# Expert blocks of 256 rows become 57 of 256 and 21 of 128, with an expert's weights packed side by side in DRAM

## The chip, the cores and the metric

The kernel runs on one core of a Trainium2 chip. A core has five engines that run their own instruction lists: PE (TensorE, matrix products into PSUM; its weight loads are listed apart as PEld), DVE (VectorE), ACT (ScalarE), POOL (GpSimd) and SP (SyncE, which here only issues transfers). The transfers themselves run on 16 DMA engines. The metric is the device time of one execution in microseconds, from which a profile of one execution is taken as well.

## The reference

A layer norm, then attention and a mixture of experts side by side, both added to the input. The input has 32 sequences of 256 rows of 128 numbers (8192 rows), all in f32.

```python
def attention(xn, Wqkv, Wproj, bproj):      # 16 heads of 8, rotary, window of 64, causal
    q, k, v = heads(xn @ Wqkv.T); q, k = rotary(q), rotary(k)
    attn = softmax(where(allow, q @ k.T / sqrt(8), -inf))
    return merge(attn @ v) @ Wproj.T + bproj

def experts(xn, gate_w, gate_b, w1, b1, w2, b2):   # 8 experts, hidden 512
    weights, indices = top_k(xn @ gate_w.T + gate_b, 2)
    weights = softmax(weights)
    out = 0
    for e in range(8):
        w_e = sum(weights * (indices == e), keepdims=True)
        h = gelu(xn @ w1[e] + b1[e])          # erf form
        out = out + w_e * (h @ w2[e] + b2[e])
    return out

xn = layernorm(x)
return x + attention(xn) + experts(xn)
```

## The kernel before

Each row goes to two of the eight experts, so 16,384 rows of expert work have to be spread. The kernel sorts rows by expert through DRAM and works them off in blocks.

**Attention** (class `Attention`) takes the sequences one after another, four turns each (`run`, L787 to L862); turn (z, r) is the r-th of sequence z. PE's order is written by hand. Beside it runs the generator `beside` (L1037), which `turn` (L805) advances once per turn: it puts normalisation, routing, sorting, experts and collecting between the attention's instructions. Steps that `yield False` go on in every turn; those that `yield True` take a share of a small budget.

SP's queue is in order. In turn (z, 1) it gets the four `km` loads of the next sequence, in (z, 2) the four `qm` loads (`alone`, L574), each set of 32 KB transfers waiting for the rotated k or q from DVE (`rk`, `rq`, L571).

**Routing and sorting.** `route` (L306), four times for a quarter of the rows each, finds each row's two experts and its place (`slot`) in the expert's region of `xs_d` in DRAM, `ER` = 8192 + 256 rows per expert. `scatters` (L1070) sends rows there with indirect DMAs from POOL, two a turn; a row of `xs_d` is 130 numbers: 128 of the row, then the row of `ys_d` to which its result goes, and its weight. When the last quarter is routed, `blocks` (L378) computes from the region ends how many blocks of 256 each expert has and, for 71 blocks, the expert (`exps[0]`) and the first row (`exps[1]`); `fills` (L1051) writes 256 void rows behind each region. 71 blocks suffice for any routing: 64 full ones and 7 more for the rests; unused ones work on void rows.

**The experts** (`experts`, L909) come when all scatters are out, in one piece, with attention standing still in between. For block b:

- `load(b)` (L916), on SP: two numbers are read into registers (expert e, first row r), then four transfers: `xg` (256 rows, 130 KB), `w1` (256 KB, 2 KB per partition), `w2` (256 KB, four runs of 512 B per partition), `b2` (one row broadcast to 128 partitions, 64 KB). The tiles have 5 buffers each; four blocks are loaded before the first, then block b + 4 is requested after the down of block b - 1.
- `turn(b)` (L935): two PE transposes into `pxg`, a DVE copy to `xT` (L940), a small DVE copy of the target rows and weights to `at` (L942, 4 buffers).
- `up(b)` (L945): four products of 128x128 weights with 256 columns into `ph` (L952; f32, two instructions each), ACT gelu with the bias of the block's expert to `h` (L958).
- `down(b)` (L964): eight products with `h` as weights and 128 columns each (L970, 16 instructions) into `po` (one PSUM buffer); DVE adds `b2` (L975) and multiplies by the weight (L976); POOL sends the two halves with indirect DMAs to the rows of `ys_d` that `at` names (L981).

PE's order of one iteration is: transposes of b + 1, up of b, down of b - 1. In the profile w1 and w2 are both called `w`, `b2` is `b`, the result tile is `yg`.

**Collecting** (`collect`, L1010): back in attention's turns, SP reads `ys_d` in order, POOL adds it to `x`, SP writes the output.

Of the kernel before, what the change touches and what calls it, by code (L numbers as in the profile page):

```python
# [12 lines left out]
I32 = mybir.dt.int32  # L13
# [18 lines left out]
NB = 71  # L32
ER = 8192 + BT
# [17 lines left out]
C_ROW = C_BLK + NB  # L51
C_VOID = C_ROW + 128
C_ALL = C_VOID + 30
# [3 lines left out]
def constants():  # L57

    f = np.float32
    c = np.zeros((P, C_ALL), f)  # L60
    p = np.arange(P)
    e = np.arange(NE)
    c[:, C_PRE : C_PRE + P] = p[:, None] < p[None, :]
    c[:, C_TIE : C_TIE + NE] = NE - e
    c[:, C_NUM : C_NUM + NE] = e
    c[:, C_BLK : C_BLK + NB] = np.arange(NB)
    c[:, C_ROW : C_ROW + 128] = p[:, None] + P * np.arange(128)[None, :]
    c[:, C_BASE : C_BASE + NE] = ER * e
    c[:, C_RUN : C_RUN + 17 * NE] = np.arange(17 * NE) % 17 > 0
    v = np.arange(30)[None, :]  # L70
    c[:, C_VOID : C_VOID + 30] = 2 * 8192 + BT * (v // 2) + 2 * p[:, None] + v % 2

    r = (p % HB)[:, None]
    k = np.arange(2 * HB)[None, :]
    ok = (k >= r) & (k <= r + WIN)
    c[:, C_MQ : C_MQ + 2 * HB] = np.where(ok & (k >= HB), f(0), f(NEG))
    c[:, C_MQ + 2 * HB : C_MQ + 4 * HB] = np.where(ok, f(0), f(NEG))

    q = np.arange(HB)[None, :]
    c[:, C_MK : C_MK + HB] = np.where(q >= r, f(0), f(NEG))  # L80
    c[:, C_MK + HB : C_MK + 2 * HB] = np.where(q <= r, f(0), f(NEG))
    c[:, C_MK + 2 * HB : C_MK + 3 * HB] = NEG
    for i in range(4):
        at = C_PICK + HB * i
        c[:HB, at : at + HB] = np.eye(HB, dtype=f)
        c[HB + 3 * i : HB + 3 * i + 3, at : at + HB] = 1
    half = HD // 2
    inv = f(1.0) / f(ROPE_BASE) ** (np.arange(half, dtype=f) / f(half))
    freq = np.arange(T, dtype=f)[None, :] * inv[p % 32 // 8][:, None]
    c[:, C_COS : C_COS + T] = np.cos(freq)  # L90

    c[:, C_SIN : C_SIN + T] = np.sin(freq) * np.where(p % 8 < 4, f(-1), f(1))[:, None]
    return c, np.zeros((P, 2 * P), f)
# [3 lines left out]
def tile_layer(  # L97
# [23 lines left out]
    NI = NB - 2 * B * T // BT  # L121
# [68 lines left out]

    xs_d = tc.dram_tile([NE * ER + NI * BT, ROW], F32, name="xs_d")
    ys_d = tc.dram_tile([2 * B * T + (NE + NI) * BT, D], F32, name="ys_d")
# [185 lines left out]
    def blocks(rt, misc):  # L378
# [4 lines left out]
        def temp(name, shape, dtype=F32):  # L383
            return rt.tile(shape, dtype, tag=name, name=name)

        after, base = run[:, :, GN], c[:, C_BASE : C_BASE + NE]
        nc.vector.tensor_copy(ends, after[0:1, :])
        nb_i = temp("nb_i", [P, NE], I32)
        nc.vector.scalar_tensor_tensor(nb_i, after, float(BT - 1), base, ALU.add, ALU.subtract)
        nc.vector.tensor_single_scalar(  # L390
            nb_i, nb_i, BT.bit_length() - 1, ALU.arith_shift_right
        )
        nb = temp("nb", [P, NE])
        nc.vector.tensor_copy(nb, nb_i)

        f = temp("f", [P, 3, NE])
        nc.vector.tensor_tensor_scan(f[:, 1, :], ones[:, 0:NE], nb, 0.0, ALU.mult, ALU.add)
        nc.vector.tensor_sub(f[:, 0, :], f[:, 1, :], nb)

        idle = NE * ER - (NB - NI) * BT  # L400
# [3 lines left out]
        nc.vector.tensor_scalar_add(f[:, 2, :], f[:, 2, :], -float(idle))  # L404
        yield False
        pf = misc("pf")
        for k in range(3):
            nc.tensor.matmul(
                pf[0:NE, k : k + 1], lhsT=f[:, k, :], rhs=ident[:, 0:1], start=True, stop=True
            )  # L410
        nc.tensor.matmul(
            pf[0:NE, 3:4], lhsT=c[:, C_NUM : C_NUM + NE], rhs=ident[:, 0:1], start=True, stop=True
        )
        fT = temp("fT", [NE, 4])
        nc.vector.tensor_copy(fT, pf[0:NE, 0:4])

        blk = c[0:NE, C_BLK : C_BLK + NB]
        oh = temp("ohb", [NE, NB])
        nc.vector.tensor_scalar(oh, blk, fT[:, 0:1], None, ALU.is_ge)
        nc.vector.scalar_tensor_tensor(oh, blk, fT[:, 1:2], oh, ALU.is_lt, ALU.mult)  # L420
        yield False
        pn = misc("pn")
        for k in range(2):
            nc.tensor.matmul(
                pn[0:1, k * NB : (k + 1) * NB], lhsT=fT[:, 3 - k : 4 - k], rhs=oh,
                start=True, stop=True,
            )
# [3 lines left out]
        for k in range(NHC):  # L431
# [7 lines left out]
        at = temp("at", [1, NB])  # L439
        nc.vector.tensor_scalar(  # L440
            at, c[0:1, C_BLK : C_BLK + NB], float(BT), float(idle), ALU.mult, ALU.add
        )
        nc.vector.tensor_add(exps[:, 1, :], at, nums[:, 1, :])
# [465 lines left out]
    def experts():  # L909
        with (  # L910
# [5 lines left out]
            def load(b):  # L916
                e = nc.sync.value_load(exps[0:1, 0, b : b + 1], min_val=0, max_val=NE - 1)
                r = nc.sync.value_load(
                    exps[0:1, 1, b : b + 1], min_val=0, max_val=NE * ER + (NI - 1) * BT
                )  # L920
                x = wt.tile([P, 2, ROW], F32, tag="xg", name=f"xg{b}")
                nc.sync.dma_start(
                    out=x, in_=xs_d[bass.ds(r, BT), :].rearrange("(p n) d -> p n d", n=2)
                )
                a = wt.tile([P, H], F32, tag="w1", name=f"w1_{b}")
                nc.sync.dma_start(out=a, in_=w1[bass.ds(e, 1), :, :].rearrange("o d h -> (o d) h"))
                z = wt.tile([P, NHC, D], F32, tag="w2", name=f"w2_{b}")
                nc.sync.dma_start(
                    out=z, in_=w2[bass.ds(e, 1), :, :].rearrange("o (k p) d -> p (o k) d", p=P)
                )  # L930
                bias = wt.tile([P, D], F32, tag="b2", name=f"b2_{b}")
                nc.sync.dma_start(out=bias, in_=b2_d[bass.ds(e, 1), :].to_broadcast([P, D]))
                return x, a, z, bias

            def turn(b, x):  # L935
                pt = misc(f"pxg{b}")[:, 0:BT]
                for n in range(2):
                    nc.tensor.transpose(pt[:, n * P : (n + 1) * P], x[:, n, 0:D], ident)  # L938
                xT = io.tile([P, BT], F32, tag="xT", name=f"xgT{b}")
                nc.vector.tensor_copy(xT, pt)  # L940
                at = io.tile([P, 2, 2], I32, tag="at", name=f"at{b}", bufs=4)
                nc.vector.tensor_copy(at, x[:, :, D:].bitcast(I32))  # L942
                return xT, at

            def up(b, xT, a):  # L945
                h = hid.tile([P, NHC, BT], F32, tag="h", name=f"h{b}")
                for k, tag in ((0, "sh"), (2, "sl")):
# [3 lines left out]
                    for j in range(2):  # L951
                        nc.tensor.matmul(  # L952
                            ph[:, j * BT : (j + 1) * BT],
                            lhsT=a[:, (k + j) * P : (k + j + 1) * P], rhs=xT,
                            start=True, stop=True,
                        )
                    for j in range(2):
                        nc.scalar.activation(  # L958
                            h[:, k + j, :], ph[:, j * BT : (j + 1) * BT], AF.Gelu,
# [4 lines left out]
            def down(b, h, z, bias, at):  # L964
                po = ps_y.tile([P, 4, P], F32, tag="y", name=f"po{b}").rearrange(
                    "p s t -> p (s t)"
                )[:, 0 : 2 * D].rearrange("p (n d) -> p n d", n=2)
                for n in range(2):
# [5 lines left out]
                y = io.tile([P, 2, D], F32, tag="y", name=f"yg{b}", bufs=4)  # L974
                nc.vector.tensor_add(y, po, bias.unsqueeze(1).to_broadcast([P, 2, D]))  # L975
                nc.vector.tensor_mul(  # L976
                    y, y, at[:, :, 1:2].bitcast(F32).to_broadcast([P, 2, D])
                )
                for n in range(2):
# [10 lines left out]
            ahead = [load(b) for b in range(4)]  # L990
            yield
            yield
            (xT, at), last = turn(0, ahead[0][0]), None
            for b in range(NB):
                x, a, z, bias = ahead.pop(0)
                now, to = xT, at
                if b + 1 < NB:
                    xT, at = turn(b + 1, ahead[0][0])
                h = up(b, now, a)
                if last is not None:  # L1000
                    down(*last)
                if b + 4 < NB:
                    ahead.append(load(b + 4))
                last = (b, h, z, bias, to)
# [32 lines left out]
    def beside():  # L1037

        rt = early.enter_context(tc.tile_pool(name="rt", bufs=1))
        void = rt.tile([P, NE, 2, ROW], F32, tag="void", name="void")  # L1040
        nc.gpsimd.memset(void, 0.0)

        def fill(first, n):

            at = C_VOID + 2 * first
            nc.gpsimd.tensor_copy(
                void[:, 0:n, :, D].bitcast(I32),
                c[:, at : at + 2 * n].rearrange("p (n k) -> p n k", k=2),
            )

        def fills():  # L1051
# [3 lines left out]
            for e in range(NE):  # L1055
                end = nc.sync.value_load(
                    ends[0:1, e : e + 1], min_val=ER * e, max_val=ER * (e + 1) - BT
# [3 lines left out]
                        out=xs_d[bass.ds(end, BT), :].rearrange("(p n) d -> p n d", n=2),  # L1061
                        in_=void[:, e],
# [29 lines left out]
        def go_on(entry):  # L1092
            entry[2] = next(entry[1], None)
            if entry[2] is None:
# [7 lines left out]
                out=xs_d[rows : rows + NI * BT, :].rearrange("(j p n) d -> p j n d", p=P, n=2),  # L1102
# [5 lines left out]
        while next(transfers, transfers) is not transfers:  # L1108
# [3 lines left out]
            if (z, r) == (1, 1):  # L1112
                begin("masks1", att.masks(1))

# [68 lines left out]
```

## Time and profile before

| what | value |
|---|---|
| median of 4 runs | 795.41 us (792.66, 792.78, 798.04, 798.21) |
| profiled execution | 791.79 us, span 790.0 us, granted clock 0.991 |
| PE busy | 732.2 us, 93% |
| PEld busy | 477.4 us, 60% |
| DVE busy | 498.6 us, 63% |
| ACT busy | 381.2 us, 48% |
| POOL busy | 413.6 us, 52% |
| first transpose of the experts to the last down's end | 359.42 to 632.31 us |
| DMA queue of SP (q1) | 117,344 packets, 79.64 MB |
| DMA queue of POOL (q0) | 8,640 packets, 17.84 MB |

The slices of a page cut the span into 40 equal parts and give the busy share in tenths. A line of a timeline has the start in us, the time from the first start to the last end of the merged instructions, engine, line, operation, output and inputs, how many were merged, and in brackets the idle time before and what ended it. Starts and ends of matmuls overlap, since they are pipelined; a step's time is read from start to start. A line of the waits has the waiting instruction, what it waited for, total us, times, and the longest.

### The profile page before, as it was taken

The numbers are of one execution on the slowest core, as the hardware profiler recorded it, in microseconds if no ns is written. First come the engines' busy times: TensorE is split into PE (matmuls) and PEld (weight loads), VectorE is DVE, ScalarE is ACT, GpSimd is POOL, SyncE is SP. The second block draws the span as 40 slices with busy tenths as digits, with TensorE's granted clock in tenths as the row PEclk, the third lists the DMA queues.
The fourth block names the chain that finished last, engine by engine and source line by source line (L and its number), as shares of the span: only waits on it lengthen the run. The fifth ranks groups of instructions, "written<-read, shape, count | busy, mean of one in ns | idle before, by whom it ended". The sixth has DMA issues, their size and how long they took to land.

```text
span 790.0 us, 20453 instructions
## 1 busy us (share of the span) xinstructions
PE 732.2 (93%) x7524; PEld 477.4 (60%) x7524; DVE 498.6 (63%) x1163; ACT 381.2 (48%) x695; POOL 413.6 (52%) x668
## 2 busy tenths in 40 slices
PE   3899989999989999998999999999999999999995
PEld 2344444444444444446999998999999944444442
DVE  3658968898887888874333433333333377878763
ACT  4256455465556454454444444444444444454543
POOL 2301568567878737781555555555555544444300
PEclk9999989999999999999999999999999999999999
DMA  4700111111112101316887888887887355436100
GB/s 134 203 24 8 49 38 52 51 39 54 59 42 65 56 28 51 119 55 198 226 233 224 230 228 241 229 246 231 222 245 228 105 146 150 141 106 169 42 22 15
DMA packets 126372, 98.87 MB, mean 125 GB/s; under 512 B 14648, under 2 KB 112600, under 8 KB 126272
## 3 DMA queue, kind: packets, MB, share of 16 engines
q1 hardware_dynamic: 117344, 79.64, 36.1%
q0 software_dynamic: 8640, 17.84, 6.5%
q8 instruction: 60, 0.98, 0.5%
q14 instruction: 40, 0.33, 0.1%
q10 hardware_dynamic: 288, 0.08, 0.0%
HBM read 65.09 MB, written 24.02 MB: 113 GB/s over the span
## 4 chain that ended last, share of the span: by engine, by line
PE 64%; DVE 14%; ACT 10%; DMA 4%; issue 3%; SPq 2%; POOL 2%; DVEq 0%; ACTq 0%; POOLq 0%
PE po L970 14%; PE ph L952 14%; PE sl L703 8%; ACT pr L713 7%; PE sl L689 7%; PE sh L634 6%; DVE mx L648 4%; PE sh L622 4%; PE y L725 4%; ACT xn L283 2%; PE pxg L938 2%; PE pm L672 1%; PE pg L295 1%; DMA ys_d<-yg,at 1%; DVE yt L734 1%
## 5 line engine op out<-in xcount | busy, mean ns | idle before, releaser
L713 ACT ACTIVATE pr<-sl 128x1024 f32<-128x1024 f32 x128 | 130.7, 1022 | 193.1 <-PE sh L634 184.9
L981 POOL DMA_INDIRECT ys_d<-yg,at x142 | 137.2, 967 | 131.1 <-DVE yg L976 98.9
L648 DVE TENSOR_REDUCE mx<-sh 128x8 f32<-128x1024 f32 x128 | 156.3, 1221 | 69.8 <-PE sh L634 69.4
L958 ACT ACTIVATE h<-ph,b_b 128x256 f32<-128x256 f32 x284 | 116.4, 470 | 147.8 <-PE ph L952 147.8
L634 PE MATMUL sh<-km,rq 32*64 32x512 f32 x1024 | 148.6, 641 | 0.5 <-DMA km<-rk 0.5
L457 POOL DMA_INDIRECT xs_d<-xn,slot x128 | 127.2, 994 | 35.8 <-issue 19.2
L703 PE MATMUL sl<-qm,rk 32*64 32x256 f32 (+1 forms) x1280 | 142.6, 485 | 0.0
L970 PEld LDWEIGHTS po<-w,h 128*128 128x128 f32 x1136 | 138.0, 192 | 4.3 <-issue 0.7
L970 PE MATMUL po<-w,h 128*128 128x128 f32 x1136 | 138.4, 275 | 0.6 <-issue 0.6
L952 PE MATMUL ph<-xgT,w 128*128 128x256 f32 x568 | 135.9, 383 | 0.6 <-DVE xgT L940 0.4
L952 PEld LDWEIGHTS ph<-xgT,w 128*128 128x128 f32 x568 | 103.3, 192 | 12.4 <-DVE xgT L940 0.7
L689 PE MATMUL sl<-rs,pick_i 76*64 76x512 bf16 x512 | 80.4, 390 | 26.2 <-ACT pr L713 20.8
L975 DVE TENSOR_TENSOR yg<-po,b 128x256 f32<-128x256 f32 x71 | 30.2, 425 | 84.7 <-PE po L970 80.9
L725 PE MATMUL y<-pr,vst 128*32 128x128 f32 (+1 forms) x1536 | 70.1, 315 | 1.0 <-DVE yt L734 1.0
L703 PEld LDWEIGHTS sl<-qm,rk 32*64 32x64 f32 x1280 | 47.9, 131 | 37.9 <-issue 29.1
L942 DVE COPY at<-xg 128x4 int32<-128x4 int32 x71 | 14.3, 202 | 83.9 <-issue 60.4
L725 PEld LDWEIGHTS y<-pr,vst 128*32 128x32 f32 x1536 | 40.1, 110 | 44.3 <-issue 39.0
L677 ACT COPY rs<-pm 12x1024 bf16<-12x1024 bf16 x63 | 60.2, 1000 | 10.8 <-PE pm L672 10.3
L689 PEld LDWEIGHTS <-pick_i 76*64 76x64 bf16 x512 | 26.9, 108 | 58.7 <-issue 46.5
L622 PE MATMUL sh<-mq,unit 64*64 64x512 bf16 x512 | 54.4, 414 | 4.1 <-DVE mx L648 3.7
L622 PEld LDWEIGHTS <-unit 64*64 64x64 bf16 x512 | 15.7, 104 | 57.7 <-issue 57.3
L734 DVE STREAM_TRANSPOSE yt<-y 128x512 f32<-128x512 f32 x64 | 45.3, 708 | 4.5 <-PE y L725 4.5
(143 smaller groups left out, 845.2 us busy)
## 6 DMA issues: line engine op xcount, KB each, us to landing
w<-in_L_ffn_w_dram SPq DMA_DIRECT2D x142, 256.0 KB
xg<-xs_d SPq DMA_DIRECT2D x71, 130.0 KB
yc<-ys_d SPq DMA_DIRECT2D x32, 256.0 KB
b<-b_d SPq DMA_DIRECT2D x71, 64.0 KB
qm<-rq SPq DMA_DIRECT2D x128, 32.0 KB
out_dram<-x SPq DMA_DIRECT2D x32, 128.0 KB
km<-rk SPq DMA_DIRECT2D x126, 32.0 KB
x<-in_L_attn_x_dram SPq DMA_DIRECT2D x15, 256.0 KB
```

The source lines that it names most:

```text
L457: nc.gpsimd.indirect_dma_start(out=xs_d, out_offset=bass.IndirectOffsetOnAxis(ap=slot[:, n, k : k + 1], axis=0), in_=xns[n // NT][:, n % N ...
L622: nc.tensor.matmul(ps[HB * h : HB * h + HB, ii, :, :], lhsT=unit2[half, :], rhs=mq[half, which, :].unsqueeze(1).to_broadcast([HB, 4, 2 * HB]),
L634: nc.tensor.matmul(ps[HB * h : HB * h + HB, ii, :, :], lhsT=q[r, t * HB : (t + 1) * HB], rhs=km[r, :, t * HB : (t + 2) * HB], start=False, ...
L648: nc.vector.tensor_reduce(mx, ps, AX.X, ALU.max, negate=True)
L689: nc.tensor.matmul(ps[HB * e : HB * e + HB, ii, :, :], lhsT=pick_i[:, 2 * ip + ii, :], rhs=rs[e][:, :, n * P : (n + 1) * P], start=True, s ...
L703: nc.tensor.matmul(ps[HB * e : HB * e + HB, ii, :, lo:hi], lhsT=k[r, kt * HB : (kt + 1) * HB], rhs=qm[r, :, n * P + lo : n * P + hi], star ...
L713: nc.scalar.activation(pr, ps, AF.Exp, scale=1.0 / math.sqrt(HD))
L725: nc.tensor.matmul(py[32 * i : 32 * i + 32, 2 * o : 2 * o + 2, lo:hi], lhsT=self.vsts[z % 3][:, tile_, i, o, :], rhs=q["pr", n, i // 2][:, ...
L952: nc.tensor.matmul(ph[:, j * BT : (j + 1) * BT], lhsT=a[:, (k + j) * P : (k + j + 1) * P], rhs=xT, start=True, stop=True,)
L958: nc.scalar.activation(h[:, k + j, :], ph[:, j * BT : (j + 1) * BT], AF.Gelu, bias=b1_b[:, k + j, b : b + 1],)
L970: nc.tensor.matmul(po[:, n, :], lhsT=h[:, k, n * P : (n + 1) * P], rhs=z[:, k, :], start=(k == 0), stop=(k == NHC - 1),)
L981: nc.gpsimd.indirect_dma_start(out=ys_d, out_offset=bass.IndirectOffsetOnAxis(ap=at[:, n, 0:1], axis=0), in_=y[:, n, :], in_offset=None,)
```

## The change

- The row count of a block is 256 (`BT`) for blocks 0 to 56 and 128 (`HT`) for blocks 57 to 77. `blocks` hands out whole blocks of 256 first, up to 57 over all experts, and covers what is left with half blocks; it computes both kinds' ranges, in one step more (a further `yield False`). An expert's region ends in 128 void rows instead of 256, and `fills` writes half as much.
- The order of work spreads the half blocks evenly: fifteen times three whole and a half one, six times two whole and a half one. The last block is a half one.
- A new generator `pack`, begun at turn (3, 0), copies for each expert w1, w2 and b2 (broadcast to 128 rows) into `w_d` in DRAM, 1152 numbers (4608 B) per partition: three DRAM to DRAM transfers per expert, 24 in all, on SP's queue; two in one turn, one in the next.
- `load` issues two transfers instead of four: `xg` and one tile `w` of 576 KB from `w_d`. `up` and `down` take their weights and the bias from slices of `w`, which has 5 buffers as w1, w2 and b2 had.
- `turn`, `up` and `down` take the row count from the tile: a half block has one transpose, up products of 128 columns, four down products, one scatter.

The diff, cut to its core:

```diff
-NB = 71
-ER = 8192 + BT
+NF, NHB, NHU = 57, 21, 14
+NB = NF + NHB
+HT = BT // 2
+ER = 8192 + HT
+NI = NHB - NHU
...
+    w_d = tc.dram_tile([NE, P, WROW], F32, name="w_d")
...
+        whole, halves = steps_of("whole", 0, BT), steps_of("halves", HT - 1, HT)
...
+        bounds(0, whole)
...
+        yield False
+        got = temp("got", [P, 2, NE])
+        nc.vector.tensor_single_scalar(got, f[:, 0:2, :], float(NF), ALU.min)
+        nc.vector.tensor_sub(whole, got[:, 1, :], got[:, 0, :])
+        nc.vector.scalar_tensor_tensor(halves, whole, -2.0, halves, ALU.mult, ALU.add)
+        bounds(3, halves)
...
             def load(b):
                 e = nc.sync.value_load(exps[0:1, 0, b : b + 1], min_val=0, max_val=NE - 1)
+                n = 2 if b < NF else 1
...
-                x = wt.tile([P, 2, ROW], F32, tag="xg", name=f"xg{b}")
+                x = wt.tile([P, 2, ROW], F32, tag="xg", name=f"xg{b}")[:, 0:n]
                 nc.sync.dma_start(
-                    out=x, in_=xs_d[bass.ds(r, BT), :].rearrange("(p n) d -> p n d", n=2)
-                )
-                a = wt.tile([P, H], F32, tag="w1", name=f"w1_{b}")
-                nc.sync.dma_start(out=a, in_=w1[bass.ds(e, 1), :, :].rearrange("o d h -> (o d) h"))
-                z = wt.tile([P, NHC, D], F32, tag="w2", name=f"w2_{b}")
+                    out=x, in_=xs_d[bass.ds(r, n * P), :].rearrange("(p n) d -> p n d", n=n)
+                )
+                w = wt.tile([P, WROW], F32, tag="w", name=f"w{b}")
                 nc.sync.dma_start(
-                    out=z, in_=w2[bass.ds(e, 1), :, :].rearrange("o (k p) d -> p (o k) d", p=P)
-                )
-                bias = wt.tile([P, D], F32, tag="b2", name=f"b2_{b}")
-                nc.sync.dma_start(out=bias, in_=b2_d[bass.ds(e, 1), :].to_broadcast([P, D]))
-                return x, a, z, bias
+                    out=w, in_=w_d[bass.ds(e, 1), :, :].rearrange("o p d -> (o p) d")
+                )
+                return x, w
...
                         nc.tensor.matmul(
-                            ph[:, j * BT : (j + 1) * BT],
-                            lhsT=a[:, (k + j) * P : (k + j + 1) * P], rhs=xT,
+                            ph[:, j * BT : j * BT + t],
+                            lhsT=w[:, (k + j) * P : (k + j + 1) * P], rhs=xT,
                             start=True, stop=True,
                         )
...
+            order, n = [], 0
+            for b in range(NF):
+                order.append(b)
+                while (n + 1) * NF <= (b + 1) * NHB:
+                    order.append(NF + n)
+                    n += 1
...
+        def pack():
+            for e in range(NE):
+                yield False
+                nc.sync.dma_start(out=w_d[e, :, 0:H], in_=w1[e])
+                nc.sync.dma_start(
+                    out=w_d[e, :, H : H + NHC * D].rearrange("p (k d) -> p k d", d=D),
+                    in_=w2[e].rearrange("(k p) d -> p k d", p=P),
+                )
+                yield False
+                nc.sync.dma_start(
+                    out=w_d[e, :, H + NHC * D :], in_=b2_d[e : e + 1, :].to_broadcast([P, D])
+                )
...
+            if (z, r) == (3, 0):
+                begin("pack", pack())
```

## The prediction

> **What bounds the kernel now.** I read the page's slices first, then the chain, then the expert stage by stretches, by PE and SP in order of time, and last who waits.
>
> ```profile
> PE   3899989999989999998999999999999999999995
> PEld 2344444444444444446999998999999944444442
> DMA  4700111111112101316887888887887355436100
> ```
>
> The slices show three stages: attention with routing, from slice 18 to 31 the experts (PE and its weight loads both full), then attention again. The diff works in the middle one.
>
> ```profile
> PE 64%; DVE 14%; ACT 10%; DMA 4%; issue 3%; SPq 2%; POOL 2%; DVEq 0%; ACTq 0%; POOLq 0%
> ...
> 500.00:550.00 50.00, 50.00 (x348) 47.20 (x348) 18.64 (x55) 22.31 (x55) 28.31 (x53) 1.00 0.83 235
> ```
>
> Chain by engine, and one stretch of the experts (busy PE, PEld, DVE, ACT, POOL, clock, DMA share, GB/s): PE has no gap, at full granted clock; the next fullest are the DMA engines, 0.83.
>
> ```profile
> 438.00 0.38 PE L938 MATMUL pxg<-ident,xg 128*128 128x128 f32 x2
> 438.22 1.89 PE L952 MATMUL ph<-xgT,w 128*128 128x256 f32 x8
> 439.95 1.95 PE L970 MATMUL po<-w,h 128*128 128x128 f32 x16
> 441.74 0.38 PE L938 MATMUL pxg<-ident,xg 128*128 128x128 f32 x2
> ```
>
> PE in order of time: start to start, one block is 0.22 (transposes) + 1.73 (up) + 1.78 (down) = 3.73 us. An instruction of 256 columns takes 1.73/8 = 216 ns, one of 128 takes 1.78/16 = 111 ns.
>
> ```profile
> 427.21 0.33 SPq L922 DMA_DIRECT2D xg<-xs_d  x1
> 427.74 0.33 SPq L926 DMA_DIRECT2D w<-in_L_ffn_w_dram  x1
> 428.31 0.38 SPq L928 DMA_DIRECT2D w<-in_L_ffn_w_dram  x1
> 428.93 0.33 SPq L932 DMA_DIRECT2D b<-b_d  x1
> 430.74 0.33 SPq L922 DMA_DIRECT2D xg<-xs_d  x1
> ```
>
> SP in order of time: a block's four issues and two register loads take 3.53 us, hardly less than PE's 3.73. Pairing starts, xg is issued only 2.4 to 4 us before its transposes in blocks 4 to 33. SP is a second bound close behind PE.
>
> ```profile
> 471.91 0.44 PE L938 MATMUL pxg<-ident,xg 128*128 128x128 f32 x2 [0.15 <-DMA xg<-xs_d]
> ...
> 487.92 0.44 PE L938 MATMUL pxg<-ident,xg 128*128 128x128 f32 x2 [0.87 <-DVE at L942]
> ```
>
> ```profile
> DVE at L942 <- DMA ys_d<-yg,at: 23.3, 23, 3.0
> ...
> PEld pxg L938 <- DMA xg<-xs_d: 2.1, 4, 1.1
> ```
>
> PE's few stalls in order of time, and two rows of the waits (total us, times, longest): from the transposes of block 3 (369.60) to those of block 70 (622.32) are 252.72 us, 67 x 3.73 = 249.98 of it work, so 2.7 us of stalls, at late xg loads and at late copies of `at`. That copy waits for earlier scatters to land.
>
> **The change part by part.** *Rows.* Before 71 x 3.73 = 264.9. A half block has 1 transpose, 8 up and 8 down instructions of 128 columns: 17 x 0.111 = 1.89. After: 57 x 3.73 + 21 x 1.89 = 252.3. **-12.5 us**, all on PE, the bound. The price of its up matmuls is L970's row, same shape, weights also changed every time.
>
> A rule speaks against that: the Trainium skill, "TensorE: Matmul & The Clock Gate", part 3, has weight loads overlap running matmuls only where their row groups differ, and these fill all rows. The rows here disagree: 216 ns for 256 columns and 111 for 128 leave 216 - 2 x (216 - 111) = 6 ns for anything that doesn't scale with columns.
>
> *One transfer.* SP saves two issues of about 0.57 (427.74 to 428.93 by starts): 3.53 - 1.15 = 2.4 us a load, while the mean block needs 252.3/78 = 3.23 of PE. Unmerged, 78 x 3.53 = 275 would have bound. In the compiled order each SP DMA waits for the eighth before it: two blocks in flight before, four after. So loads run ahead until a buffer is missing. The one tile w is now held until the add of its block, where w1 was free after the up: w for four blocks on is issued about 0.6 into the iteration after that add's matmuls, three iterations (9.35 at the shortest) less 0.4 ahead of its up; xg some 1.9 behind on SP, 6.9 ahead of its transposes. Both beat today's 2.4 to 4, so the load stalls go: **-2.0** of the 2.7. Without that cover each us of lateness costs up to 78.
>
> *DMA time.* Between 400 and 500 us the SP queue's share, 71.1% of 1600 engine-us for 27 blocks, is 42.1 a block. Full-load stretches give packets of 496 B 32.5 ns (20 to 30 us: 5603 at 113.7%), of 1 KB 46 (34 to 37 us), of 3.8 KB 150 (6 to 7 us: 104, 0.40 MB, 97.4%; 25.7 GB/s an engine). After: whole 128 x 46 ns + 0.59 MB/25.7 = 28.8, half 27.1; in sum 2211 engine-us for 2989. At today's 17.2 GB/s it would be 55 MB/17.2 = 3200, with 135 scatters of 2.84 still 89% of 16 x 252. No bound either way: 0.
>
> *The index ring.* `at` has four buffers: block i's copy waits for the scatters of block i-4, and behind it on DVE stands the add that frees the one PSUM buffer the next down needs. By starts, the copies of blocks 6 to 70 ran 5.07 to 8.28 us after the transposes of block i-1 (median 6.32). PE stalls only past two iterations + 1.95 - 0.6 (copy, add) = 8.8: never so far. With a half block among them iterations shrink to 2.89 and 2.84, the limit at 24 places to 7.0 to 7.1, elsewhere to 7.8 or more. Laying the 65 measured delays on these limits gives 24 x 0.1 + 0.3 = 2.7 us of stalls. A late copy delays the add and the scatters behind it, so I take **+4**; bounds 0.7 (all landing 0.5 earlier) and 16 (1.0 later).
>
> *Ends.* SP's faster first loads save 0 to 1.5 at xg 1's 1.44 us wait (the ACT table load follows); the last block's 0.56 gap has a longer down above it: **-1**.
>
> *Before the experts.* 24 pack DMAs go to SP among the km and qm issues, about 0.6 each, 14 us over 16 turns of 3.4; SP waits there 175 us for rk anyway. Their data, 5120 packets of 512 B and 1024 of 2 KB (83 ns between the rows above), is 251/16 = 16 us of DMA where the share is 0.16. A km load is issued three turns, 10 us, ahead and needs 2.4 + 2, so what stands before it (two transfers, 1.7) is hidden; without that cover up to 16. Eleven small DVE instructions of 0.11 to 0.29 in `blocks` add 2 us to an engine 85% busy there; its extra turn lies under the last 16 turns of scatters. **+1** (0 to 4). Smaller fills and 7 fewer scatters on POOL (0.97 each, POOL half idle): 0.
>
> Sum: -12.5 - 2.0 + 4 - 1 + 1 = **-10.5**. Profiled execution: 791.8 (span 790.0) - 10.5 = 781.3. The four runs lie near 792.7 and 798.1, their median 3.6 above that execution: 784.9 on that scale. I forecast **783**.
>
> **The rivals.** *A, slower: scatters land later.* Place: the ring. A load's queue will hold 8 packets of 4.6 KB an engine, about 8 x 0.18 = 1.4 us, issued just as the block's scatters go out. If a scatter stands behind all of them, delays shift by 1.0 to 1.5 and the ring's stalls are 16 to 30: from 1.0 on (12.5 + 2.0 + 1 - 1 = 14.5 to lose) it decides; at 1.5, 791.8 - 14.5 + 30 = 807. For it: landing already varies from 1.5 to 4.7 us after POOL's end. Against: 26% less DMA time, and the second scatter goes out 1.3 after the first, past the burst. The Trainium skill, "DMA: Bandwidth & Descriptors", "Queues, rings and completion order", has engines alternate between queues packet by packet; by it a scatter's two packets an engine wait 2 x 0.18, shift about 0.3, 2 us more than forecast. No row separates the two.
>
> *B, no gain: a milder shift.* At +0.7 the ring's list gives 10 us, 14 with its echo: 791.8 - 14.5 + 14 = 791.
>
> *C, the half block isn't half.* If each of its up matmuls showed a weight load as long as its own columns, up would cost a whole one's 1.73: 21 x 0.84 = +17.6, so 781.3 + 17.6 = 799. L970's row is against it.
>
> *D, more.* The lighter queue lands scatters 0.5 sooner, no load is late: -12.5 - 2.7 + 0.7 - 1.5 = -16, 776.
>
> **How the numbers follow.** Forecast (8 to 14 us less) 0.54, D 0.12, B 0.14, A 0.15, C 0.05. About 1% is what measurements of this kernel tell from no change. Faster by over that: forecast and D, 0.66; within it B and a part of A, 0.18; slower A's rest and C, 0.16. The range runs from D, 776 less the spread of runs, to A where it begins to cost: 775 to 796; the likeliest case alone gives 778 to 787.
>
> **What would show it.** Half blocks 1.89 us of PE by the timeline, ph of 128 columns at 111 ns; SP pace 2.4 and xg issued over 6 us ahead; PE idle before po or ph ending at DVE, just behind half blocks, 3 to 5 us in all; DMA share under 0.75; the stage 273 us before, 262 after; stretches before 357 us unchanged. Wrong it is if the waits of `at` on ys_d double and their longest exceeds 4 us (A), or if PE idles at km loads during the pack.

## The result and the profile after

The changed kernel takes 794.72 us (median of 42 runs, 781.55 to 808.94), the kernel before 793.79 beside it (63 runs, 789.27 to 803.39). The medians lie 0.9 us apart, the changed kernel's the longer: nothing was gained where 10.5 us were forecast. The ratio, 0.9951 with a 95% interval of [0.9929, 0.9973], takes of each kernel only the runs within 1.5% of its fastest, 15 of these 42 and 61 of these 63, and so flatters the kernel with the wider spread; the ratios further down are made the same way. The changed kernel's profiled execution took 797.46 us, span 795.7.

| us, profiled execution | before | after |
|---|---|---|
| up to the experts' first transpose | 359.4 | 361.6 (+2.1) |
| from there to the last down's end | 272.9 | 271.0 (-1.9) |
| the rest | 157.7 | 163.2 (+5.5) |
| span | 790.0 | 795.7 (+5.7) |

The slices of the changed kernel's page, busy tenths:

```profile
PE   3899989999989998998999799998999999999986
DMA  4701425111211101218877677877888355543100
```

In the expert stage PE now has a 7 and an 8 where it was full before, while DMA is no fuller. Slices 4 to 6 of DMA, counted from 0 as in the prediction, show the packing's copies. The chain by engine, then the same stretch of 50 us as before (busy PE, PEld, DVE, ACT, POOL, clock, DMA share, GB/s):

```profile
PE 54%; DVE 15%; ACT 10%; DMA 10%; issue 7%; POOL 3%; SPq 1%; DVEq 0%; POOLq 0%; ACTq 0%
```

```profile
500.00:550.00 50.00, 47.90 (x343) 44.76 (x341) 17.21 (x58) 22.71 (x62) 26.56 (x52) 1.00 0.80 246
```

PE lost ten points of the chain, DMA won six, and PE stands 2.1 of 50 us. PE in order of time, where nothing waits:

```profile
468.44 0.38 PE L971 MATMUL pxg<-ident,xg 128*128 128x128 f32 x2
468.65 1.06 PE L986 MATMUL ph<-xgT,w 128*128 128x128 f32 x8
469.55 1.95 PE L1006 MATMUL po<-w,h 128*128 128x128 f32 x16
471.33 0.38 PE L971 MATMUL pxg<-ident,xg 128*128 128x128 f32 x2
471.55 1.89 PE L986 MATMUL ph<-xgT,w 128*128 128x256 f32 x8
473.28 1.05 PE L1006 MATMUL po<-w,h 128*128 128x128 f32 x8
474.17 0.38 PE L971 MATMUL pxg<-ident,xg 128*128 128x128 f32 x2
```

By starts, the half block's up (468.65 to 469.55) takes 0.90 and its down (473.28 to 474.17) 0.89: eight instructions of 128 columns at 111 to 113 ns each. The iterations are 2.89 and 2.84 us, as worked out. And where something waits, a block behind a half one, PE, DVE and SP in order of time:

```profile
435.46 1.89 PE L986 MATMUL ph<-xgT,w 128*128 128x256 f32 x8
438.85 0.17 DVE L975 COPY at<-xg 128x4 int32<-128x4 int32 x1 [6.08 <-issue]
438.96 0.42 DVE L1011 TENSOR_TENSOR yg<-po,w 128x256 f32<-128x256 f32 x1
439.41 0.33 SPq L962 DMA_DIRECT2D w<-w_d  x1
439.42 0.42 DVE L1014 TENSOR_TENSOR yg<-yg,at 128x256 f32<-128x256 f32 x1
439.44 2.05 PE L1006 MATMUL po<-w,h 128*128 128x128 f32 x16 [2.09 <-DVE yg L1011]
```

DVE stands 6.08 us before the copy of `at` (the row names no releaser; the waits below put 43 of these copies down to scatters); the add behind it frees `po`, and the down starts 2.09 us late. The same add lets the next weights go out (439.41). The waits (waiting instruction, what for, total us, times, longest):

```profile
DVE at L975 <- DMA ys_d<-yg,at: 56.4, 43, 4.2
...
PEld po L1006 <- DVE yg L1011: 13.0, 12, 2.5
...
PE po L1006 <- DVE yg L1011: 9.3, 10, 2.1
...
PE pxg L971 <- DMA xg<-xs_d: 2.2, 1, 2.2
```

Against before, the wait for scatters went from 23.3 to 56.4 us, PE's wait behind it is new, and the one late xg load left lies in the first blocks.

### The profile page after: what moved, and what is told of

Its sections match the earlier page's. It is cut to its first block, busy times and chain, and to the rows that moved or that the text cites. A ratio compares the mean times of both kernels' runs of the same rounds, so it can differ in the third digit from the quotient of the medians.

```text
span 795.7 us, 20094 instructions
## 1 busy us (share of the span) xinstructions
PE 727.7 (91%) x7525; PEld 470.4 (59%) x7525; DVE 498.9 (63%) x1202; ACT 382.3 (48%) x723; POOL 405.5 (51%) x654
## 4 chain that ended last, share of the span: by engine, by line
PE 54%; DVE 15%; ACT 10%; DMA 10%; issue 7%; POOL 3%; SPq 1%; DVEq 0%; POOLq 0%; ACTq 0%
PE po L1006 10%; PE ph L986 9%; PE sl L737 8%; ACT pr L747 7%; PE sl L723 7%; DMA ys_d<-yg,at 6%; PE sh L668 5%; PE y L759 4%; PE sh L656 4%; DVE mx L682 4%; DMA w<-w_d 3%; ACT xn L292 2%; PE pg L304 2%; PE pm L706 1%; POOL xs_d L491 1%
## 5 line engine op out<-in xcount | busy, mean ns | idle before, releaser
L1019 POOL DMA_INDIRECT ys_d<-yg,at x135 | 130.5, 967 | 136.0 <-DVE yg L1014 61.7
L992 ACT ACTIVATE h<-ph,b_b 128x256 f32<-128x256 f32 (+1 forms) x312 | 117.5, 443 | 145.6 <-PE ph L986 145.5
L737 PE MATMUL sl<-qm,rk 32*64 32x256 f32 (+1 forms) x1280 | 144.9, 497 | 0.0
L1006 PE MATMUL po<-w,h 128*128 128x128 f32 x1080 | 135.5, 278 | 9.5 <-DVE yg L1011 9.3
L1006 PEld LDWEIGHTS po<-w,h 128*128 128x128 f32 x1080 | 131.3, 193 | 16.1 <-DVE yg L1011 13.0
L986 PE MATMUL ph<-xgT,w 128*128 128x256 f32 (+1 forms) x624 | 130.7, 353 | 1.2 <-ACT h L992 1.2
L723 PE MATMUL sl<-rs,pick_i 76*64 76x512 bf16 x512 | 82.0, 397 | 26.2 <-ACT pr L747 21.3
L975 DVE COPY at<-xg 128x4 int32<-128x4 int32 (+1 forms) x78 | 14.8, 190 | 119.4 <-issue 62.8
L1011 DVE TENSOR_TENSOR yg<-po,w 128x256 f32<-128x256 f32 (+1 forms) x78 | 30.3, 389 | 49.9 <-PE po L1006 44.4
```

Source lines behind the costliest of these rows:

```text
L723: nc.tensor.matmul(ps[HB * e : HB * e + HB, ii, :, :], lhsT=pick_i[:, 2 * ip + ii, :], rhs=rs[e][:, :, n * P : (n + 1) * P], start=True, s ...
L737: nc.tensor.matmul(ps[HB * e : HB * e + HB, ii, :, lo:hi], lhsT=k[r, kt * HB : (kt + 1) * HB], rhs=qm[r, :, n * P + lo : n * P + hi], star ...
L986: nc.tensor.matmul(ph[:, j * BT : j * BT + t], lhsT=w[:, (k + j) * P : (k + j + 1) * P], rhs=xT, start=True, stop=True,)
L992: nc.scalar.activation(h[:, k + j, :], ph[:, j * BT : j * BT + t], AF.Gelu, bias=b1_b[:, k + j, b : b + 1],)
L1006: nc.tensor.matmul(po[:, n, :], lhsT=h[:, k, n * P : (n + 1) * P], rhs=z[:, k, :], start=(k == 0), stop=(k == NHC - 1),)
L1019: nc.gpsimd.indirect_dma_start(out=ys_d, out_offset=bass.IndirectOffsetOnAxis(ap=at[:, n, 0:1], axis=0), in_=y[:, n, :], in_offset=None,)
```

## Experiments

Theory **R**: the gain is eaten by the ring of `at`. Theory **O**: a part is lost ahead of the experts. Rivals were the merged load itself (packets of 4.6 KB ahead of scatters) and the DMA engines' load. "Stalls" below are the iterations' lengths from block 4 on, less their undisturbed ones. "Landing" is the time from POOL's end of a block's last scatter to the copy of `at` four blocks on, by its median over copies that waited more than 0.3 us. Both are worked out from the timelines, the stalls to some 0.3 us.

| kernel | us, median (runs) | ratio to before, 95% | experts from | stage | stalls | landing |
|---|---|---|---|---|---|---|
| before | 793.79 (63) | 1 | 359.4 | 272.9 | 2.3 | 2.73 |
| changed | 794.72 (42) | 0.9951 [0.9929, 0.9973] | 361.6 | 271.0 | 13.4 | 2.95 |
| e1 ring 8 | 782.42 (6) | 0.984 [0.98, 0.988] | 370.7 | 257.9 | 0 | none waited |
| e2 before, ring 8 | 792.49 (10) | 0.9973 [0.9942, 1.0004] | 360.6 | 271.7 | 1.2 | none waited |
| e3 whole blocks, one transfer | 793.81 (10) | 0.998 [0.9944, 1.0015] | 361.0 | 270.2 | 0 | 2.29 |
| e5 runs of 512 B | 789.23 (10) | 0.9889 [0.985, 0.9929] | 365.6 | 260.9 | 2.8 | 2.94 |
| e7 ring 8, finer steps | 778.28 (6) | 0.98 [0.9756, 0.9845] | 360.4 | 257.3 | 0 | none waited |
| e4 ring 8, four transfers | 817.17 (4) | 1.0306 [1.0247, 1.0364] | 364.4 | 288.5 | 31.0 | none waited |
| e8 six weight buffers | 795.19 (1) | | 370.7 | 263.4 | 5.4 | 2.77 |
| e10 no later weights | 786.54 (1) | | 370.4 | 257.9 | 0 | 1.35 |
| e11 finer steps | 795.71 (4) | | 361.2 | 276.4 | 18.9 | 3.06 |
| e12 ring 5, finer steps | 777.06 (4) | 0.9796 [0.971, 0.9881] | 358.8 | 257.3 | 0 | none waited |
| e13 e7 with 512 B | 777.00 (4) | 0.9799 [0.9702, 0.9896] | 359.6 | 257.8 | 0 | none waited |
| e14 e1 again | 781.49 (4) | 0.9835 [0.9745, 0.9925] | 365.3 | 257.9 | 0 | none waited |

**The ring, in both kernels** (e1 from the changed kernel, e2 from the one before, where the line has no slice at its end).

```diff
-at = io.tile([P, 2, 2], I32, tag="at", name=f"at{b}", bufs=4)[:, 0:n]
+at = io.tile([P, 2, 2], I32, tag="at", name=f"at{b}", bufs=8)[:, 0:n]
```

> The changed kernel with 8 buffers of `at` in place of 4, nothing else. Theory R (the index ring took the gain: copies of `at` wait for scatters of four blocks back, and the add behind them holds PE): the expert stage, first transpose to the last down's end, falls from 271 us in the changed kernel's profile to 257 to 259 (its 13.4 us of excess gone), PE's waits for the add go from 22 us to under 2, and the time is 12 to 15 us under the kernel before, ratio 0.981 to 0.985. Rival O (the gain was lost outside the experts: the stage starts 2.1 us later and what follows it takes 5.5 us more than before): the stage may shorten, but the ratio stays within 0.990 to 1.0.

> The kernel before with 8 buffers of `at`. Theory R: with whole blocks alone the ring hardly binds; at most the 2.7 us of stalls go, ratio 0.996 to 1.0. If instead the ring costs all kernels alike (or 8 buffers speed something else), the ratio is 0.985 or lower, as in the changed kernel.

Eight index buffers take 13 us out of the changed kernel's expert stage and next to nothing out of the old one's. PE's only wait left at `po` in e1 is at the last two blocks:

```profile
PE po L1006 <- DVE yg L1011: 0.6, 1, 0.6
```

So R holds: the half blocks gained what was worked out, and a ring that had bound next to nothing took it back. O has a part as well: e1's experts start at 370.7 us, 11 us later than in the kernel before.

**The merged load alone** (e3): the kernel before, 71 whole blocks, with the packed weights and one transfer.

```diff
-                a = wt.tile([P, H], F32, tag="w1", name=f"w1_{b}")
...
+                w = wt.tile([P, WROW], F32, tag="w", name=f"w{b}")
+                nc.sync.dma_start(
+                    out=w, in_=w_d[bass.ds(e, 1), :, :].rearrange("o p d -> (o p) d")
+                )
...
+            if (z, r) == (3, 0):
+                begin("pack", pack())
```

> The packing and the one transfer for a block alone, 71 whole blocks, `at` with 4 buffers. It tells the size of packets from the spacing of blocks. If rows of 4608 B by themselves make scatters land later, the wait from the end of a block's second scatter to the copy of `at` four blocks on has a median of 3.0 us or more, as in the changed kernel (3.05), where before had 2.69; if it is the closer spacing, it stays near 2.7. PE limit of the ring is 8.8 us here, so stalls stay under 4 us either way, xg is issued 7 us or more ahead, and the ratio is 0.995 to 1.0. What the pack costs ahead of the experts shows in the start of the stage: 359.4 before, 361.6 in the changed kernel.

The load stalls are gone (stage 270.2 for 272.9) and scatters land sooner than before, 2.29 us for 2.73. With blocks spaced as before, packets of 4.6 KB by themselves don't make scatters late. The packing costs nothing that shows: its last transfer goes out at 133 us, and the routing's last step (`blocks`) begins at 298.3 us, in the kernel before at 298.2.

**Short packets** (e5): the changed kernel with `w_d` stored as nine runs of 512 B per partition.

```diff
-    w_d = tc.dram_tile([NE, P, WROW], F32, name="w_d")
+    w_d = tc.dram_tile([NE, 2 * NHC + 1, P, D], F32, name="w_d")
...
-                    out=w, in_=w_d[bass.ds(e, 1), :, :].rearrange("o p d -> (o p) d")
+                    out=w.rearrange("p (k d) -> p k d", d=D),
+                    in_=w_d[bass.ds(e, 1), :, :, :].rearrange("o k p d -> p (o k) d"),
...
```

> The changed kernel with the packed weights stored as nine runs of 512 B per partition: still one transfer a block, same bytes, but 1152 packets where there were 128. If large packets ahead of the scatters made them late, the median wait falls from 3.05 towards 2.7 us and the stage's excess from 13.4 to about 5 us, ratio 0.985 to 0.992. If it is the load on the queue, DMA share rises from 0.77 to 0.85 or more, the wait grows, and the ratio is 1.0 or more.

Its median lies 5.5 us under that of the changed kernel, and it stalls less, yet its scatters land no sooner (2.94 us). It met the ring's limit less often; why is not settled by this run.

**Four transfers with half blocks** (e4, eight index buffers): `load` as it was before, no packing.

> The changed kernel with eight index buffers, but four transfers a load straight from the weights, no packed copy. Theory (SP then bounds): 78 loads of 3.53 us are 275 us, against 258 of the expert stage with one transfer, so the stage takes 270 to 276 us and the time is 12 to 18 us above the 782.4 of eight buffers with one transfer, less 1 to 2 for the copies saved: 793 to 799. Rival (SP's 3.53 holds waits that shrink with the blocks): stage 258 to 262, 780 to 785.

The slowest of all, 3% behind the kernel before. SP in order of time, and the waits:

```profile
440.49 0.33 SPq L957 DMA_DIRECT2D xg<-xs_d  x1
...
442.21 0.33 SPq L967 DMA_DIRECT2D b<-b_d  x1
443.91 0.33 SPq L957 DMA_DIRECT2D xg<-xs_d  x1
```

```profile
PEld pxg L975 <- DMA xg<-xs_d: 30.0, 34, 2.3
```

A load costs SP 3.42 us (440.49 to 443.91) where the mean block needs 3.23 of PE, and SP's own waits (6.6 and 6.2 us in all, for PE's ups and downs to free weight buffers) make it 3.66 on the mean; 78 of those are 285 us of the stage's 288.5. The forecast, 270 to 276 us, had the direction right and the size too small: what an SP that is the bound has waited, it doesn't catch up. Half blocks without the merge lose.

**What makes scatters land late** (e8, e10). e8 gives the weights a sixth buffer, so that their load doesn't wait for the add (32 bytes for it come from `ends`, moved to a pool that is closed by then). In e10 the weights of the first five blocks serve all later ones; 73 loads are left out, and the experts compute with other weights.

```diff
-                w = wt.tile([P, WROW], F32, tag="w", name=f"w{b}")
+                w = wt.tile([P, WROW], F32, tag="w", name=f"w{b}", bufs=6)
```

```diff
+            held = []
...
+                if len(held) == 5:
+                    return x, held[b % 5]
                 w = wt.tile([P, WROW], F32, tag="w", name=f"w{b}")
...
+                held.append(w)
```

> The changed kernel (four index buffers) with six buffers of weights for five, so that a load's weights no longer wait for the add of the block before; nothing else in the expert stage differs. Theory (in the changed kernel the weights go out just ahead of a scatter because both follow the same add, and the scatter lands late for that): fewer than 10 of the scatters have a weight load issued under 2 us before POOL's end (34 of 74 in the changed kernel), mean landing 2.4 to 2.7 us for 3.04, stalls behind late copies of at most 6 us for 13.4. Rival (the distance doesn't matter, or the load is then held by the copy of the index tile, which stands just before the same add): landing 2.9 to 3.2, stalls 10 to 15 us.

> The changed kernel (four index buffers) in which the weights of only the first five blocks are loaded and later blocks use those again: 73 transfers of 0.59 MB are left out, everything else stays, so the experts' results are of other weights. Theory (a weight load close ahead of a scatter makes it land late): mean landing 1.8 to 2.3 us for 3.04, stalls behind late copies of at most 2 us for 13.4, the stage 257 to 260 us. Rival (the landing is the scatter's own, the shorter iterations alone set the stalls): landing 2.7 or more, stalls 6 us or more.

Without the loads scatters land 1.35 us after POOL's end, no copy stalls PE, and of the waits for scatters (56.4 us) this is left:

```profile
DVE at L980 <- DMA ys_d<-yg,at: 13.8, 14, 1.4
```

So in the changed kernel the weight loads double a scatter's landing (2.95 us for 1.35). The kernel before, with as many bytes of weights a block, has 2.73; that the loads do it there too was not run. That distance in time decides was not shown: in the changed kernel scatters that POOL finished less than 2 us after a weight load went out landed in 3.4 us on the mean (34 of 61), later ones in 2.5, but e8 left 39 of 63 that close and still has 5.4 us of stalls for 13.4. In the kernel before, distance made no difference (2.86 and 2.89).

**Ahead of the experts** (e7, e11, e14). The changed kernel before its experts, POOL, DVE and PE in order of time:

```profile
298.38 0.17 DVE L418 TENSOR_TENSOR f<-f,whole 128x8 f32<-128x8 f32 x1
298.59 1.99 DVE L421 SCALAR_TENSOR_TENSOR f<-f,c 128x8 f32<-128x8 f32 x1
299.12 0.62 PE L723 MATMUL sl<-rs,pick_i 76*64 76x512 bf16 x4 [0.15 <-issue]
299.27 1.27 POOL L598 TENSOR_TENSOR rotq<-rotq,c 128x512 f32<-128x512 f32 x1
300.50 1.21 DVE L682 TENSOR_REDUCE mx<-sh 128x8 f32<-128x1024 f32 x1
301.76 0.49 PE L656 MATMUL sh<-mq,unit 64*64 64x512 bf16 x4 [2.02 <-DVE mx L682]
```

One of `blocks`' small instructions takes 1.99 us and ends with POOL's product (300.58 and 300.54); attention's reduction stands behind it, and PE behind that. The kernel before counts in one step of seven instructions, the changed one puts ten into the first. Stretches of the changed kernel (clock third from the end):

```profile
302.00:306.00 4.00, 4.00 (x37) 2.09 (x33) 3.66 (x13) 1.63 (x4) 2.38 (x5) 0.58 0.07 25
306.00:310.00 4.00, 4.00 (x71) 2.25 (x67) 3.79 (x13) 1.50 (x3) 2.63 (x4) 1.00 0.20 62
```

Behind the gap the granted clock falls to 0.58 for one stretch. In e1, with the same gap, it stays low for three (0.54, 0.50, 0.68). What this costs can be read from the first instruction of `blocks` to the experts' first transpose: 61.2 us in the kernel before (from 298.2), 64.4 in the changed kernel (from 297.1), 68.8 in e1 (from 301.9), and 64.4 to 68.9 in all seven profiles with ten instructions in the first step. Of the 9 us by which e1's experts start later than the changed kernel's, 4.3 lie behind the counting's start; the 4.8 ahead of it no run explains. e7 is e1 with the counting cut finer, so that a step has at most seven small instructions:

```diff
+        yield False
         bounds(0, whole)
...
-        yield False
 
         got = temp("got", [P, 2, NE])
...
+        yield False
         bounds(3, halves)
```

> The changed kernel with eight index buffers, and the routing's block counting cut one step finer, so that no step of it puts more than 7 small instructions on DVE (the kernel before: 7, the changed one: 10 in the first step). Theory (the first step's tenth instruction, 1.99 us where its like takes 0.17, runs into POOL's product of two tiles and ends with it; PE stands 2.0 us behind it and the granted clock falls after that): no instruction of the counting over 0.4 us, no PE gap over 1 us between 290 and 310 us, the experts' first transpose at 360 to 364 us for 370.7 with eight buffers, the median 2 to 7 us under that kernel's 782.4, so 775 to 780. Rival (the clock falls there by chance, the gap is only 2 us of it): start at 366 to 370, median 780 to 782. Rival (one more step moves the experts by a turn): no gain, 782 to 785.

> The changed kernel with the block counting cut one step finer and its four index buffers kept. Theory (two separate losses: the gap ahead of the experts with the clock's fall behind it, and the ring): the experts start at 360 to 362 us, the granted clock between 300 and 320 us is 1.00, stalls behind late copies stay at 3 to 14 us, median 786 to 792. Rival (the gap is the smaller part and the ring eats what it gives): 792 to 796.

> The changed kernel with eight index buffers and its block counting as it was, again, beside the finer counting with five. Theory (the gap ahead of the experts and the clock's fall behind it cost 2 to 7 us): 3 to 6 us above five buffers with the finer counting, 780 to 785. Rival (the 4 us between the two earlier jobs were chance): within 2 us of it.

In e7 no instruction of the counting takes over 0.34 us, the PE gap at that place is 0.69, and the clock stays full:

```profile
302.00:306.00 4.00, 3.17 (x34) 1.62 (x20) 3.79 (x12) 1.70 (x4) 3.57 (x7) 1.00 0.20 66
306.00:310.00 4.00, 3.95 (x76) 2.34 (x82) 3.73 (x14) 2.44 (x3) 2.34 (x4) 1.00 0.21 62
```

Its experts start at 360.4 us, 61.5 us after the counting's first instruction; in all four profiles with the finer step it is 61.5 to 61.7. e14, which keeps the coarse step, is 4.4 us above e12 of the same job, and e1 was 4.1 above e7. The intervals of the ratios overlap, so the 4 us are likely rather than certain; that the gap goes with the step, and with it 3 to 7 us ahead of the experts, is seen directly. The clock's fall has other causes too: in e3, which counts as the kernel before does and whose PE waits nowhere over 0.6 us between 280 and 330 us, it fell as well.

```profile
306.00:310.00 4.00, 4.00 (x45) 1.78 (x44) 1.82 (x4) 1.02 (x1) 2.07 (x4) 0.58 0.13 37
```

e11, the finer step with four index buffers, missed its forecast of 786 to 792 and came out where its rival had it, 792 to 796: start and clock are mended as expected, but 18.9 us of stalls at the ring are in its profile. Its runs are 779.32, 795.50, 795.92 and 798.95: the ring's price differs from run to run, and the first may have escaped it (no profile shows that one); no ratio is drawn from so wide a spread. The changed kernel's 42 runs spread over 27 us, the old kernel's 63 over 14.

**How deep the ring must be, and packets again** (e12: five buffers, finer steps; e13: e7 with e5's layout).

> The changed kernel with the finer block counting and five index buffers. Theory (a fifth buffer gives a copy one iteration more, at least 2.84 us on limits of 7.0 and up, so 9.9, and past that only the odd delay of 10 to 11 reaches): stalls behind late copies 0 to 1 us, stage 257 to 258.5, median as with eight, 776 to 781. Rival (lateness feeds on itself and takes the fifth buffer too): stalls 3 us or more, median 782 or more.

> Eight index buffers, the finer block counting, and the packed weights in nine runs of 512 B per partition instead of one of 4608 B. Theory (packet size reached the time only through the landing of scatters, and eight buffers make that immaterial): stage 257 to 258.5, ratio to before within 0.5% of five buffers' in this job. Rival (short packets are better in themselves, as the four-buffer version with them was 0.6% ahead): 3 us or more under it. Rival (they cost DMA time, so that loads come late): stage over 259.

One buffer more is enough: no copy in e12 waits for a scatter, the stage is 257.3 us. With that, the packets' size is worth nothing (777.00 beside 777.06), so what e5 gained, it gained at the ring. e7, e12 and e13 beat both kernels by 2%; e7 has the narrowest interval. Its chain is PE's again:

```profile
PE 67%; DVE 14%; ACT 10%; issue 4%; POOL 3%; DMA 1%; SPq 1%; DVEq 0%; ACTq 0%; POOLq 0%
```

## Why the prediction failed

**Rows (-12.5), load stalls (-2.0), ends (-1): right.** The stage without ring stalls is 257.3 to 257.9 us for 272.9, so -15.0 to -15.6 for -15.5. Half blocks take 1.90 us for 1.89. Rival C is out; so is the rule of the Trainium skill ("TensorE: Matmul & The Clock Gate", part 3) that spoke for it: these weights fill all rows and their loads don't show. SP's first loads come 2.22 to 2.28 us apart (2.4 forecast), xg goes out 4.5 to 10.5 us ahead, mostly 7, where I had said at least 6.9.

**DMA time (0): right in effect, wrong in its figures.** Between 400 and 600 us the SP queue's share is 68.3%, 2186 engine-us for about 57.6 blocks of 3.47 us: 38 a block, not 27 to 29. That is 40.8 MB at 18.7 GB/s an engine, near the 17.2 of the kernel before, the other value I gave. The DMA share was 0.78 there, over my 0.75. It bound nothing: e10 without the loads has e1's stage.

**The ring (+4): the step that failed, by its size.** Place and chain of waits are as described: copy, add, `po`, just behind half blocks. Measured were 13.4 us in this profile and 18.9 in e11's, within and past my bounds of 0.7 and 16. Landing moved little, by 0.2 us (2.73 to 2.95; means over all copies 2.82 and 3.10); my list prices that at about 5. What the list lacked is the echo, for which I added 1.3 us: it laid delays of a kernel that never stalled on shorter limits, as if a late copy had no consequence. A late copy makes the add late, the add the scatter and the next weights, the scatter the copy four blocks on. The longest delay grew from 8.28 to 10.9 us. The echo can be read off against e1, the same kernel without a stall: measured against PE's transposes three blocks on, POOL ends a block's scatters 0.49 us later than in e1 on the mean, and 1.8 to 3.4 us later ahead of the five longest delays (9.4 to 10.9 us), whose own landings, 3.8 to 5.3 us, were long too. How much of the 13.4 us is echo and how much long landings was not separated, and why the same limit cost only 2.8 us in e5 and 5.4 in e8 stays open.

**Rival B named the outcome, but with a milder cause.** It needed 0.7 us later landing for 10 us of stalls; 0.2 to 0.3 was enough for 13.4. A's cause, weight loads that make scatters late, is real (e10), but a landing of 2.73 us before speaks for most of it having been there already. Its sign of warning came: waits of `at` doubled, the longest 4.2 us. The rule of the Trainium skill that I set beside it ("DMA: Bandwidth & Descriptors", "Queues, rings and completion order", queues served packet by packet) gave a shift of 0.3 by my estimate, which took each packet in the profile for one packet of that rule. A shift of 0.2 to 0.3 was measured; but e3, with the same packets, lands 0.4 sooner, so the agreement proves nothing.

**Before the experts (+1, 0 to 4): too small.** The packing costs nothing that shows (e3). Missed were the ten instructions in one step: I counted their own 0.11 to 0.29 us, not that one can stand behind POOL. The start moved by 2.1 us in the profiled execution, by 5 to 11 in others with that step; counted from the first instruction of `blocks` it is 3.2 us in the profiled execution and up to 7.7 in others. The median is some 4 us worse for it.

**The scale.** I put the median 3.6 above the profiled execution. Here it lay 2.7 below, since 5.5 us of that execution are lost near its end. PE there, the changed kernel:

```profile
772.43 0.38 PE L723 MATMUL sl<-rs,pick_i 76*64 76x512 bf16 x1 [2.02 <-ACT rs L711]
773.15 1.87 PE L723 MATMUL sl<-rs,pick_i 76*64 76x512 bf16 x7 [0.35 <-DVE rs L711]
```

And the kernel before, the same instructions:

```profile
772.87 0.38 PE L689 MATMUL sl<-rs,pick_i 76*64 76x512 bf16 x1 [2.02 <-ACT rs L677]
773.59 1.02 PE L689 MATMUL sl<-rs,pick_i 76*64 76x512 bf16 x7 [0.35 <-DVE rs L677]
```

The wait of 2.02 us is in both; behind it the granted clock fell in one execution (0.62 and 0.50 over 772 to 780 us) and not in the other (1.00). It is no effect of the change: e3, with whole blocks, lost 4.6 us there, while the ten other profiles with half blocks take 156.4 to 159.7 us behind the experts, where the kernel before takes 157.7.

In medians: 777.1 (e12) is what is left with neither loss. It lies where rival D put it (776), but by luck: D wanted scatters to land 0.5 us sooner, and here a fifth buffer took the stalls away. The coarse step adds about 4 us and the ring about 13, which gives 794, near the 794.7 measured. The two losses don't simply add, though: e11, with the ring's alone, has 795.7.

## What to carry to other kernels

Before work is cut into smaller pieces, list every ring that turns once per piece, also those with no wait to their name, and count its release in pieces of the new length; when a buffer of 16 bytes per partition is all it takes, add one. Don't lay the delays of a kernel that never stalls on tighter limits: once a limit is met, lateness returns through the ring. And small instructions put beside finished work are priced by the engine that waits behind them, not by their own duration.

## What the hardware showed

A DVE instruction with two operands in SBUF that is worth 0.17 us took 1.98 or 1.99 beside POOL's product of two tiles, in all seven profiles with ten instructions in the first step. The kernel before has the same elsewhere: `yn` (L754) takes 2.17 us at 329.67 and 0.42 in other turns, and POOL's L564 runs from 330.27 to 331.55. The Trainium skill, "SBUF — State Buffer", "Who interferes with whom", says that a DVE instruction with two SBUF inputs contends with a GpSimd instruction that reads SBUF, and that the ports they share are an exclusive lock. The ends agree, 0.04 and 0.29 us apart. The starts are less clear: in the profile DVE begins 0.68 and 0.60 us ahead of POOL's product and is yet the one that stands, and no run here settles why.

In those seven profiles PE waited 2.02 us, and in that wait or at most 6 us after it the granted clock fell, in its lowest stretch of 4 us to between 0.50 and 0.79. In the four with the finer step PE waited 0.67 to 0.81 us at that place and the clock stayed at 1.00. A wait of 2 us is neither needed nor enough, though: in e3 the clock fell to 0.58 without one, and in the kernel before it stayed at 1.00 behind the one that ends at 772.87 us. The Trainium skill, "TensorE: Matmul & The Clock Gate", Part 1, puts the fall after an idle window of about 3.4 us. These rows show it behind shorter waits; no run here varied the wait's length to find the bound.
